# Images 1 to 3's scan inputs made on a clock, and two backward results kept apart in every phase

## The chip, the core and the metric

The kernel runs on one core of a Trainium2 chip. Its engines work side by side, each through its own instructions in order: PE (TensorE, matrix products), DVE (VectorE), ACT (ScalarE), POOL (GpSimd) and SP (SyncE, which here issues the DMAs). The metric is the device time of one execution in microseconds. Three runs of the kernel before gave 5556.42, 5560.28 and 5569.84 us; their median, 5560.28, is the time before.

## The reference

Four images of 64 x 64 positions with 96 channels go through four layers. What matters here is the first, a two-dimensional selective scan:

```python
xz = x @ W_in.T; xp, z = xz[..., :192], xz[..., 192:]
xc = silu(conv3x3(xp) + conv_b)                     # 192 -> 192 channels
xs = four orders of the 4096 positions: rows, columns, and both reversed
dts, Bs, Cs = split(x_proj(xs));  delta = softplus(dt_proj(dts) + dt_b)
h_t = exp(delta_t * A) * h_{t-1} + delta_t * u_t * B_t   # 192 channels x 16 states
y_t = sum over the 16 states of h_t * C_t
out = (sum of y over the four orders, + D * u) * silu(z) @ W_out.T
```

Then come a depthwise and a pointwise convolution, a linear attention with a quantised feed-forward, and a filter by Fourier transforms with another feed-forward. All of it is 32-bit but for the feed-forwards.

## The kernel before

**Scans.** A scan instruction of DVE runs the recurrence along 1024 positions (a chunk; four make an image) for 128 rows, which are 8 channels x 16 states. An image has 24 such groups (NG), a group is a unit, and a unit has two phases: the even one ("row") scans along rows, the odd one along columns, over a copy of B that ACT has turned (Bc, L1628). There are N = 192 phases and eight steps in each. In steps 0 to 3 chunks 0 to 3 are scanned forward into tiles S (L1959), in steps 4 to 7 chunks 3 to 0 backward (L1966). ACT makes the decays exp(delta * A) into two PSUM tiles "pa" just ahead (decay, L1669 and L1675): one each at steps 0 to 2 and at steps 5, 6 and 7.

A backward result can go two ways. As a rule it overwrites its decay in pa, and DVE adds it to the forward one (L1977), after a copy of its first column as the next chunk's start (L1976); POOL then multiplies the sum by C (times_c, L1658) and PE adds up the 16 states into PSUM (reduce, L1691: four matmuls of 512 columns for each chunk, as the profile counts them). For a chunk listed in apart[n] it goes into B's own tile instead, nothing is added, and POOL and PE treat it as a further result. At the unit's end ACT copies the one PSUM bank "py" out (L1698). The function plan(n) lays down at which step of the phase each of these is issued. Before the change apart[n] is (3,) as long as the flag "pre" is not set, and (3, 2) afterwards.

**Five S tiles** serve all phases in turn, so a forward scan waits until PE has reduced what stood there before. One step is 2.7 to 3.6 us.

**The other work** goes in between. After each step the function pieces(step) gives each engine a credit (gains, in estimated us: PE, ACT, POOL, DVE, SP) and lets the waiting streams issue while the credit lasts; streams are Python generators that yield the cost of what they issue next, NEXT (not before the next step) or LONG (only at step 12 of 16). clock[0] counts the steps. There are two lanes, served in this order. The side lane turns the column scans' results back (turn_back) and adds up an image's four orders (post: L648, L675). The main lane (main_lane) first makes the scan inputs of images 1, 2 and 3 one after the other, then sets done["pre"], then takes images 0, 1 and 2 through the other layers (rest). Image 0's inputs are made ahead of the scans. After the scans the lanes are emptied, and image 3's rest follows alone.

**The scan inputs** (before_scans) of an image are eight blocks of 512 positions, through five streams: project (load x, normalise on ACT in tile xb at L317, PE products into padded tiles "low" and "high"), project_z, convolve (30 products a block, L393), gates (silu and softplus on ACT; the two silus, at L508 and L509, stand behind LONG and need two loads of the activation table), and scan_inputs (four POOL operations for each half, L576 to L584, and the stores). Streams hold each other up by counts of finished blocks. While "pre" is not set the credits are multiplied by (0.9, 1.05, 1.25, 1, 1); in the last 24 phases, POOL's and SP's by 1.25.

**The rest of an image** in order: layer 1 (L937), layer norms (L1038 to L1108), attention (L1125, L1198), feed-forward (L1225, L1234, L1245), Fourier stages (L1299 and L1321, L1378, L1427, L1466), layer norm, feed-forward.

Of the kernel before, what the change touches and what calls it, by code (L numbers as in the profile page):

```python
# [24 lines left out]
NG = DI // 8  # L25
RK = 6
BLK = 512
NBLK = L // BLK
# [19 lines left out]
NCH = L // CH  # L48
NEXT = "next"
LONG = "long"  # L50


class Region:
# [20 lines left out]
def layers(ctx: ExitStack, tc: tile.TileContext, a: dict, out):  # L74
# [36 lines left out]
    clock = [0]  # L111
# [11 lines left out]
    def steps_past(since, n):  # L123

        while ordered[0] and clock[0] < since + n:
            yield NEXT
# [8 lines left out]
    done = {}  # L135
# [35 lines left out]
    def rows_of(i):  # L171

        r0 = RPB * i
        return r0, max(r0 - 1, 0), min(r0 + RPB + 1, HW)
# [40 lines left out]
    def until(ready):  # L215
        while not ready():
            yield NEXT
# [43 lines left out]
    def before_scans(b, wk, take, deep=1, prev=None):  # L261
# [5 lines left out]
        pairs = b == 0  # L267

        def count(stage):

            before = NBLK if prev is None else done[stage, prev]
            return done.get((stage, b), 0) + before - NBLK
# [18 lines left out]
        def project():  # L291

            yield from until(lambda: b in norm and count("z") > -2)
            gn = norm[b]

            def load_x(i):
                _, lo, hi = rows_of(i)
                xb = wk.tile([C, RPB + 2, HW], F32, tag="xb", name="xb", bufs=2)
                nc.sync.dma_start(
                    xb[:, : hi - lo, :],  # L300
                    x[:, lo * HW : hi * HW].rearrange("p (r w) -> p r w", w=HW),
                )
                return xb, clock[0]

            nxt = load_x(0)
            for i in range(NBLK):
                yield from until(
                    lambda: i - len(padded) < count("conv") and i - 2 < count("z")
                )
                r0, lo, hi = rows_of(i)  # L310
                n = hi - lo
                yield NEXT
                xb, since = nxt
                yield from steps_past(since, LANDING)
                yield (0, 0.9, 0, 0)
                xbs[b, i] = xb
                nc.scalar.activation(  # L317
                    xb[:, :n, :], xb[:, :n, :], AF.Identity, scale=gn[:, 0:1], bias=gn[:, 1:2]
                )
                low, high = xps[b, i] = padded[i % len(padded)]  # L320
                if i == 0 or i == NBLK - 1:
                    edge = 0 if i == 0 else RPB + 1
                    nc.gpsimd.memset(low[:, edge, :], 0.0)
                    nc.gpsimd.memset(high[: 128 if pairs else 64, edge, :], 0.0)
                at = lo - r0 + 1
                for c in range(2):
                    for ra, rb in ((0, 5), (5, n)):
                        p, give = yield from take("p_xp", 128, (rb - ra) * HW)
                        yield (0.8, 0, 0, 0)
                        nc.tensor.matmul(  # L330
                            p, lhsT=w_twice if c else w_in[:, :128], rhs=xb[:, ra:rb, :],
                            start=True, stop=True,
                        )
                        yield NEXT
                        yield (0, 0.84 if c else 0.42, 0, 0)
                        rows = p.rearrange("p (r w) -> p r w", w=HW)
                        if c == 0:
                            nc.scalar.copy(low[:, at + ra : at + rb, 1 : HW + 1], rows)
                        else:
                            nc.scalar.copy(high[:64, at + ra : at + rb, 1 : HW + 1], rows[:64])  # L340
                            if pairs:
                                nc.scalar.copy(
                                    high[64:, at + ra : at + rb, :HW], rows[64:]
                                )
                                give()
                                continue

                            ja, jb = max(at + ra - 1, 0), min(at + rb - 1, RPB)
                            nc.scalar.copy(
                                high[64:, ja:jb, 1 : HW + 1],  # L350
                                rows[64:, ja + 1 - at - ra : jb + 1 - at - ra, :],
                            )
                        give()
                done["project", b] = i + 1
                if i + 1 < NBLK:
                    yield from until(lambda: i - 1 < count("z"))
                    yield (0, 0, 0, 0, 1)
                    nxt = load_x(i + 1)
# [140 lines left out]
        def gates():  # L499

            for i in range(NBLK):
# [3 lines left out]
                sz = szs.pop((b, i))  # L505
                yield LONG
                flush()
# [1069 lines left out]
    N = 2 * len(units)  # L1577
    dls, Bs, Bcs, Ss, gs, reps, rep_cols = {}, {}, {}, {}, {}, {}, {}
    pys, yss = {}, {}
    apart = {}  # L1580

    def phase(n):

        b, g = units[n // 2]
        return b, g, n % 2
# [177 lines left out]
    def pieces(step):  # L1763

        clock[0] += 1
        assert clock[0] % 16 == (step + 1) % 16
        for free, bank in returned:
            free.append(bank)
        returned.clear()
        for e in range(5):  # L1770

            more = 1.25 if e in (2, 4) and clock[0] > 8 * (N - NG) else 1
            if "pre" not in done:
                more = (0.9, 1.05, 1.25, 1, 1)[e]
            credit[e] = min(cap[e], credit[e] + gains[step][e] * more)
        for lane in list(lanes):
            if not lane.live():
                lanes.remove(lane)
                continue
            for s in list(lane.streams):  # L1780
                while s[1] is not None:
                    if s[1] == NEXT:
                        if s[2] == clock[0]:
                            break
                        lane.advance(s)
                        continue
                    if s[1] == LONG:
                        if step != 12:
                            break
                        cost = (0, 5.0, 0, 0)  # L1790
                    else:
                        cost = s[1]
                        if any(
                            c > 0 and credit[e] < min(c, cap[e]) - 0.5 for e, c in enumerate(cost)
                        ):
                            break
                    for e in range(len(cost)):
                        credit[e] -= cost[e]
                    lane.advance(s)
                if s[1] is None:  # L1800
                    lane.streams.remove(s)
# [91 lines left out]
    def plan(n):  # L1893

        t, u = 8 * n, n // 2
        two = "pre" in done
        apart[n] = (3, 2) if two else (3,)
        row = n % 2 == 0
        b, g, _ = phase(n)
        last, first = g == NG - 1, g == 0  # L1900

        if row:
            for q, k in ((0, 7), (1, 8), (2, 9), (3, 10)):
                at(t + k, load_du, u + 1, q)
            for q, k in ((0, 3), (1, 5), (2, 15), (3, 16)):
                at(t + k, load_delta, u + 1, q)
            if last:
                for q in range(NCH):
                    at(t + 2 + q, load_rep, b + 1, 0, q)
                for q, k in ((3, 8), (2, 9), (1, 11), (0, 12)):  # L1910
                    at(t + k, load_rep, b + 1, 1, q)
            for q, k in ((3, 2), (2, 3), (1, 4), (0, 6)):
                at(t + k, copy_b, u, q)
            if first:
                for q in range(NCH):
                    at(t + 6 + q // 2, copy_rep, b, q)
        else:
            for q, k in ((0, 2), (1, 3), (2, 6 if two else 5), (3, 9)):
                at(t + k, times_b, u + 1, q)

        if two:
            order = ((2, False, 4, 6), (3, False, 5, 6), (3, True, 6, 7), (2, True, 7, 8))
        else:
            order = ((3, False, 4, 6), (2, False, 6, 7), (3, True, 7, 8))
        end = (0, False, 9, 10) if row else (0, False, 11, 12)
        for q, back, k, r in (*order, (1, False, 8, 9), end):
            at(t + k, times_c, n, q, back)
            at(t + r, reduce, n, q, back)
        if not row:
            at(t + 13, result, u)  # L1930
            for j in range(4):
                at(t + 14 + j, store_result, u, j)

    with tc.manual_schedule():
# [4 lines left out]
        for step in range(8 * N):  # L1939
            n, k = divmod(step, 8)  # L1940
            if k == 0:
                plan(n)
                if n % (2 * NG) == 2 * NG - 2 and n // 2 + 1 < len(units):
                    b = units[n // 2 + 1][0]
# [11 lines left out]
            if k < 4:  # L1956
                q = k
# [5 lines left out]
            else:  # L1963
                q = 7 - k
# [159 lines left out]
```

## Time and profile before

| | |
|---|---|
| median of three runs | 5560.28 us |
| profiled execution | 5556.72 us |
| its span | 5554.8 us |
| granted PE clock, mean | 0.805 |
| first to last scan | 290.6 to 5109.2 us |
| after the last scan | 445.6 us |
| adds at L1977 | 441 |
| backward scans into B / Bc | 163 / 164 |

The profile lists busy time by engine, groups of equal instructions with their count, busy time and mean, and the idle time ahead of them with what ended it ("POOL S L1658 <- DVE S L1959" is POOL waiting for the scan that writes S). A stretch is a window of the execution with each engine's busy time and number of instructions in it. Since every step has one scan, the number of scans started before an instruction gives its step, eight to a phase.

### The profile page before, as it was taken

Reading aid. Unit: us, or ns where it says so; the run is one execution under the profiler, and the core shown is the slowest. Engines: PE = TensorE matmul, PEld = TensorE weight load, DVE = VectorE, ACT = ScalarE, POOL = GpSimd, SP = SyncE. Lnnn points to the kernel's source line nnn. Section 1 sums busy time; section 2 is a strip of 40 time slices with the busy share of each in tenths; the row PEclk is TensorE's granted clock in tenths of the full one; section 3 lists DMA queues with packets and bytes.
Section 4 is the critical chain, followed back from the end, with each engine's and each line's share of the span. In section 5 each row is a group of like instructions: output and inputs, shape, how many; then the busy total and the mean of one; then the engine's idle time right before and its main releaser. Section 6 shows DMA issues by size and latency. Waiting matters only on the chain. (4 is left out here: it accounts for less than half of the span.)

```text
span 5554.8 us, 60794 instructions
## 1 busy us (share of the span) xinstructions
PE 4365.4 (79%) x20542; PEld 1597.5 (29%) x20542; DVE 4634.1 (83%) x3114; ACT 3563.4 (64%) x4542; POOL 3971.1 (71%) x1966
## 2 busy tenths in 40 slices
PE   7977888978888887787758876877478767786878
PEld 4422222222222221254202211542012213451346
DVE  4278988788778999999989999999899999997464
ACT  5767767777677567666675667576655676565233
POOL 1358777777777778878887789787887797786100
PEclk9978888988888877678768876797578867886888
DMA  4334443433355633436446434363465335463012
GB/s 128 97 110 115 115 123 107 135 114 115 113 148 157 184 100 92 120 114 194 135 136 181 119 96 120 113 197 107 135 175 152 97 101 165 149 182 109 7 56 95
DMA packets 298092, 694.68 MB, mean 125 GB/s; under 512 B 58184, under 2 KB 95156, under 8 KB 297652
## 3 DMA queue, kind: packets, MB, share of 16 engines
q1 hardware_dynamic: 297780, 690.80, 44.0%
q8 instruction: 162, 2.65, 0.2%
q14 instruction: 150, 1.23, 0.1%
HBM read 564.22 MB, written 126.35 MB: 124 GB/s over the span
## 5 line engine op out<-in xcount | busy, mean ns | idle before, releaser
L1658 POOL TENSOR_TENSOR S<-S,rep 128x1024 f32<-128x1024 f32 x768 | 1807.4, 2362 | 748.1 <-DVE S L1959 586.9
L1691 PE MATMUL py<-S,red 128*32 128x512 f32 x3072 | 947.6, 786 | 497.7 <-POOL S L1658 320.0
L1675 ACT ACTIVATE pa<-dl,nega 128x512 f32<-128x512 f32 x1152 | 791.1, 689 | 530.6 <-DVE Bc L1966 268.0
L1669 ACT ACTIVATE pa<-dl,nega 128x1024 f32<-128x1024 f32 x576 | 641.9, 1115 | 456.8 <-DVE S L1977 221.9
L1653 POOL TENSOR_TENSOR B<-B,rep 128x1024 f32<-128x1024 f32 x384 | 901.8, 2357 | 22.0 <-DMA B<-du_s 15.5
L1959 DVE TENSOR_TENSOR_SCAN S<-pa,S,Bc 128x1024 f32<-128x1024 f32 x288 | 676.0, 2347 | 179.3 <-PE py L1691 79.1
L1959 DVE TENSOR_TENSOR_SCAN S<-pa,S,B 128x1024 f32<-128x1024 f32 x288 | 676.0, 2347 | 142.1 <-ACT pa L1669 63.1
L1628 ACT COPY Bc<-B 128x1024 f32<-128x1024 f32 x384 | 747.7, 2009 | 16.2 <-POOL B L1653 11.9
L1977 DVE TENSOR_TENSOR S<-S,pa 128x1024 f32<-128x1024 f32 x441 | 535.9, 1215 | 6.6
L393 PE MATMUL p_conv<-low,conv_w 128*96 128x512 f32 x864 | 427.3, 647 | 31.3 <-ACT u L405 30.9
L1658 POOL TENSOR_TENSOR B<-B,rep 128x1024 f32<-128x1024 f32 x163 | 385.6, 2369 | 45.5 <-DVE pa L1966 22.4
L1691 PEld LDWEIGHTS py<-S,red 128*32 128x32 f32 x3072 | 118.8, 121 | 1036.1 <-POOL S L1658 580.8
L1966 DVE TENSOR_TENSOR_SCAN B<-pa,B 128x1024 f32<-128x1024 f32 x163 | 377.7, 2317 | 17.4 <-ACT Bc L1628 2.3
L1658 POOL TENSOR_TENSOR Bc<-Bc,rep 128x1024 f32<-128x1024 f32 x164 | 385.0, 2361 | 6.6 <-DVE Bc L1966 3.7
L1966 DVE TENSOR_TENSOR_SCAN Bc<-pa,Bc 128x1024 f32<-128x1024 f32 x164 | 379.3, 2313 | 4.5
L1966 DVE TENSOR_TENSOR_SCAN pa<-pa,edge,Bc 128x1024 f32<-128x1024 f32 x124 | 291.6, 2352 | 38.8 <-ACT pa L1675 38.8
L1234 POOL CAST h<-y 128x1536 fp8e5<-128x1536 f16 x64 | 96.0, 1500 | 305.0 <-ACT y L869 289.8
L1691 PE MATMUL py<-Bc,red 128*32 128x512 f32 x656 | 231.5, 809 | 104.1 <-POOL Bc L1658 104.0
L1966 DVE TENSOR_TENSOR_SCAN pa<-pa,edge,B 128x1024 f32<-128x1024 f32 x125 | 293.8, 2350 | 9.3 <-ACT pa L1669 9.2
L393 PE MATMUL p_conv<-high,conv_w 64*96 64x512 f32 (+1 forms) x576 | 274.7, 612 | 0.0
L1691 PE MATMUL py<-B,red 128*32 128x512 f32 x652 | 204.9, 709 | 61.8 <-POOL B L1658 61.8
L1966 DVE TENSOR_TENSOR_SCAN pa<-pa,B 128x1024 f32<-128x1024 f32 x96 | 226.1, 2356 | 26.3 <-ACT pa L1669 22.6
(274 smaller groups left out, 7409.2 us busy)
## 6 DMA issues: line engine op xcount, KB each, us to landing
dl<-delta_s SPq DMA_DIRECT2D x770, 256.0 KB
B<-du_s SPq DMA_DIRECT2D x768, 256.0 KB
z_s<-z SPq DMA_DIRECT2D x48, 512.0 KB
zl<-z_s SPq DMA_DIRECT2D x64, 384.0 KB
side<-y_s SPq DMA_DIRECT2D x112, 192.0 KB
rep<-bc_s SPq DMA_DIRECT2D x64, 256.0 KB
tw<-in_dft SPq DMA_DIRECT2D x64, 256.0 KB
side<-in_xT SPq DMA_DIRECT2D x64, 192.0 KB
```

Source lines behind the costliest of these rows:

```text
L393: nc.tensor.matmul(p, lhsT=conv_w[: src.shape[0], k, oc * C : (oc + 1) * C], rhs=src[:, ky : ky + RPB, kx : kx + HW], start=(k == 0), stop ...
L1234: nc.gpsimd.tensor_copy(h, y, saturate=False)
L1628: nc.scalar.copy(dst.rearrange("p (w h) -> p h w", h=HW)[:, q * h : (q + 1) * h, :], src.rearrange("p (h w) -> p h w", w=HW),)
L1653: nc.gpsimd.tensor_tensor(Bs[u, q], Bs[u, q], reps[units[u][0], 0, q], ALU.mult)
L1658: nc.gpsimd.tensor_tensor(t, t, c_of(n, q), ALU.mult)
L1669: nc.scalar.activation(pa, dls[u, q // 2][:, at : at + CH], AF.Exp, scale=scale)
L1675: nc.scalar.activation(to[:, k * HW // 2 : (k + 1) * HW // 2, :], src[:, :, q * w : (q + 1) * w], AF.Exp, scale=scale,)
L1691: nc.tensor.matmul(py[32 * j : 32 * j + 32, :], lhsT=red[:, 24 - 8 * s : 56 - 8 * s], rhs=x[:, k * BLK : (k + 1) * BLK], start=s == 0 and ...
L1959: nc.vector.tensor_tensor_scan(s, pas[q], b_of(n, q), Ss[n, q - 1][:, CH - 1 : CH] if q else 0.0, ALU.mult, ALU.add,)
L1966: nc.vector.tensor_tensor_scan(to[:, ::-1], pas[q][:, ::-1], b_of(n, q)[:, ::-1], edge if q < 3 else 0.0, ALU.mult, ALU.add,)
L1977: nc.vector.tensor_tensor(Ss[n, q], Ss[n, q], to, ALU.add)
```

## The change

- A constant PRE_STEPS = 470. In project, block i of image b (1 to 3) may not begin before step 470 x ((b - 1) x 8 + i) / 24, besides the conditions that it had.
- apart[n] is (3, 2) in every phase, and plan lays down the order of that case always.
- In the last 24 phases PE's credit too is multiplied by 1.25.

```diff
+PRE_STEPS = 470
...
             nxt = load_x(0)
             for i in range(NBLK):
+                turn_of = 0 if pairs else PRE_STEPS * ((b - 1) * NBLK + i) // (3 * NBLK)
                 yield from until(
                     lambda: i - len(padded) < count("conv") and i - 2 < count("z")
+                    and clock[0] >= turn_of
                 )
...
-            more = 1.25 if e in (2, 4) and clock[0] > 8 * (N - NG) else 1
+            more = 1.25 if e in (0, 2, 4) and clock[0] > 8 * (N - NG) else 1
             if "pre" not in done:
                 more = (0.9, 1.05, 1.25, 1, 1)[e]
...
         t, u = 8 * n, n // 2
-        two = "pre" in done
-        apart[n] = (3, 2) if two else (3,)
+        apart[n] = (3, 2)
...
-            for q, k in ((0, 2), (1, 3), (2, 6 if two else 5), (3, 9)):
+            for q, k in ((0, 2), (1, 3), (2, 6), (3, 9)):
                 at(t + k, times_b, u + 1, q)
 
-        if two:
-            order = ((2, False, 4, 6), (3, False, 5, 6), (3, True, 6, 7), (2, True, 7, 8))
-        else:
-            order = ((3, False, 4, 6), (2, False, 6, 7), (3, True, 7, 8))
+        order = ((2, False, 4, 6), (3, False, 5, 6), (3, True, 6, 7), (2, True, 7, 8))
```

(An entry of order is the chunk, whether it is the backward result, the step of POOL's multiply and the step of PE's reduction.)

## The prediction

> **What bounds the kernel now.** I read the page's first two parts, then a table of stretches cut at the starts of phases (a phase is eight scans on DVE; its start is the start of its first scan, which reads no S), then DVE's waits, then single stretches of the timeline.
>
> ```profile
> span 5554.8 us, 60794 instructions
> PE 4365.4 (79%) x20542; PEld 1597.5 (29%) x20542; DVE 4634.1 (83%) x3114; ACT 3563.4 (64%) x4542; POOL 3971.1 (71%) x1966
> ```
>
> No engine is full over the span. The stretches differ (columns: us, then busy us of PE, weight load, DVE, ACT and POOL, then PE clock and DMA):
>
> ```profile
> 404.30:711.70 307.40, 257.60 (x615) 68.38 (x614) 267.32 (x156) 226.64 (x286) 239.99 (x124) 0.84 0.41 117
> 711.70:1161.00 449.30, 392.57 (x938) 112.86 (x936) 356.46 (x210) 330.23 (x432) 338.82 (x178) 0.87 0.41 119
> 1366.00:1598.00 232.00, 205.07 (x481) 59.03 (x480) 178.15 (x105) 163.88 (x212) 169.86 (x89) 0.85 0.45 128
> 1743.90:1986.90 243.00, 192.92 (x502) 51.68 (x501) 228.38 (x144) 146.81 (x169) 197.64 (x93) 0.87 0.63 174
> 404.30:1986.90 1582.60, 1348.90 (x3241) 374.19 (x3240) 1319.87 (x780) 1135.90 (x1433) 1210.79 (x620) 0.86 0.45 129
> 1986.90:5109.20 3122.30, 2324.88 (x12978) 871.93 (x12976) 2911.85 (x1722) 2050.38 (x2545) 2553.74 (x1176) 0.76 0.48 134
> ```
>
> These are phases 4-15, 16-31, 40-47, 53-62, 4-62 and 63-191: 25.6, 28.1, 29.0, 24.3, 26.8 and 24.2 us a phase. From phase 63 on DVE is busy 93% and is the bound. Up to phase 56, while the inputs of images 1 to 3 are made, DVE is busy 22.3 us of 25 to 29 and waits for others:
>
> ```profile
> DVE S L1959 <- PE py L1691: 86.5, 31, 4.6
> DVE S L1959 <- ACT pa L1669: 75.8, 44, 23.2
> DVE pa L1966 <- ACT pa L1675: 38.1, 19, 4.0
> ```
>
> (290.6 to 1839.9 us.) The engines run in order, so PE's reductions stand behind the convolution, ACT's decays behind evacuations that wait for PE. In the dense stretch (phases 40-47) PE is busy 88%.
>
> **Where the input blocks lie.** Counting scans gives each row a step (eight a phase). The 24 blocks' first ACT rows (xb, L317) lie at steps 5, 10, 24, 42, 58, 81, 105, 126, then mostly 16 apart up to 398; the last POOL row of an input (L584) is at step 450. The flag is therefore set in phase 56: 441 adds at L1977 are 384 + 57, three in each of 57 phases and two in the other 135.
>
> **Part a, the clock.** Block j may not start before step 470j/24, so blocks come every 19.6 steps, the last at 450 or later; with the 52 steps from 398 to 450 the inputs end near step 502, phase 62. The wait is in the order of issue; no engine waits in it. Its DMAs, two PE stages, ACT and POOL work move with it, same number. Prices by stretch: phases 4-15 had blocks at 42, 58, 81, 105 and 126, 21 steps apart, and cost 25.6 us with (257.60 - 77.68)/12 = 15.0 us of PE other than the reductions (77.68 is line L1691's busy time there). Phases 16-31, 16 apart, cost 28.1 with (392.57 - 93.33)/16 = 18.7. A block is thus 39 us of PE; at 19.6 steps it is 39.2 x 8/19.6 = 16.0 a phase, and 25.6 + 1.0 x (28.1 - 25.6)/3.7 = 26.3 us. 59 phases (4 to 62) at 26.3 are 1552 against 1582.6: **-31**. At 25.6 it is -72; at the old 26.8, nothing.
>
> **Part b, two results apart.** In 57 phases one add goes, with its copy of the edge: a scan ended at 1384.63 and the next began at 1385.86, so 1.23 us, at most 70 in all. But ACT must have the next decay ready:
>
> ```profile
> 1413.89 1.21 DVE L1977 TENSOR_TENSOR S<-S,pa 128x1024 f32<-128x1024 f32 x1
> 1416.89 2.36 DVE L1966 TENSOR_TENSOR_SCAN pa<-pa,edge,Bc 128x1024 f32<-128x1024 f32 x1 [1.79 <-ACT pa L1675]
> ```
>
> Here ACT was in the two silus with their table loads (1410.83 to 1415.44), and without the add DVE would only wait longer. There is one such turn for each of 24 blocks, so 33 of 57 phases keep the gain: -41. Added are 57 POOL multiplies of 2.36 us (rows L1658) and 57 reductions, 1.33 us each ((231.5 + 204.9)/(656 + 652) a matmul, four to each), 76 us of PE. A block's PE time costs (28.1 - 25.6)/3.7 = 0.67 us per us with its ACT and POOL work; a reduction brings PE alone, so I take half, 0.33: +25. Zero and the full 76 are the ends. POOL's need becomes 20.0 + 2.36 + about 0.3 = 22.7 us a phase; it was busy 173.1 of 192.1 us (90%) at 3274.8 to 3466.9, at 24.0 us a phase, so it is no bound at 26: 0. The multiply of B's chunk 2 goes from step 5 to 6 of the odd phase, its scan comes four steps later: 0. B's chunk 2 is freed at step 8 instead of 5, and SP loads into it at step 10; later phases do the same with 8.5 us of such waits by POOL: 0; if the cover goes, SP's later loads queue behind it. Sum **-16**, ends -70 and +76.
>
> **Part c, what the inputs now meet.** Image 0's sums (L648, L675) run at steps 426 to 494. Until now the convolution (L393) ended at 426. Now three blocks fall among them. The sums cost 187.5 x 96/336 + 72.5 x 32/112 = 74 us of PE; 52 of their 62 steps now lie beside convolutions, 62 us. No row shows both. Alone on PE they would cost 0.33 a us, as a dense block 0.67; the middle gives **+31**, ends 0 and 47 (0.75, from phases 40-47).
>
> **Part d, image 0's layer 1** (L937, 68 us of PE: (128.5 + 75.6)/3) stood at steps 457 to 513, paced by the sums; it now starts near 503 with its input complete, and catches up. It ran partly in phases 57-62, which part a has priced anew, so some of its cost comes back: 0 to 23 (0.33), taken **+6**. The rest of the image ended at step 790 and image 1's began at 830, so a delay of up to 40 steps goes no further.
>
> **Part e, PE's 1.25 in the last 24 phases.** Image 2's Fourier stages ran slower there than image 1's: L1299 took 58 steps (1377-1435) against 43, beside image 3's sums. With a quarter more PE credit I expect some 20 steps back, which brings in what was left over at the end: four of its eight last feed-forward blocks ran after the scans, with 4.4 + 5.3 + 5.1 = 14.8 us of PE between 5107 and 5200 (L1225, L1245, L1108) while PE was 98% busy (24.44 of 25, 5150 to 5175). **-15**, and +3 for what the scans then carry; ends -20 and +10.
>
> **Sum**: -31 - 16 + 31 + 6 - 12 = -22 on the profiled execution's 5556.7 us (span 5554.8 and 1.9 around it), 5535. That execution lies 3.6 under the median of 5560.3: **5538 us**. A change within 0.3% (17 us) is what a measurement can hardly tell from none.
>
> **Rivals.** (1) *PE becomes the bound* (slower). Phases 4-62 hold 1348.9 us of PE, 355.8 of them L1691's; less the sums' 74 and some 40 of layer 1 the inputs are 879, and some 18 move in from phases 0-3. The new load is 897 + 74 + 59 x 7.45 of reductions (1006.0/135 phases, L1691 after 1839.9) = 1411 us. At the 85.2% that PE reached there (1348.9/1582.6) it takes 1655, +72; with d and e +66: **5626**. It decides below 89%. For it: 88% is the most that any long stretch of inputs held, and PE is what DVE waits for first. Against it: the 88% stood where the order of issue was crowded; at 21 steps 25.6 us sufficed.
>
> (2) *Everything takes.* 25.6 a phase (-72), all adds saved less the reductions (-45), no cost in c and d, -15: **5428**. Against it: the silu turns.
>
> (3) *No effect*: crowding goes from early phases to phases 53-62, and b nets nothing: **5560**, within 17.
>
> (4) *A colder PE.* The row first: after 6.2 us without work, 12 convolution matmuls took 8.02 us, 0.67 each; 6 soon after took 2.82, 0.47.
>
> ```profile
> 1385.66 1.92 PE L1691 MATMUL py<-S,red 128*32 128x512 f32 x4 [6.22 <-ACT ys L1698]
> 1387.51 2.02 PE L544 MATMUL p_dt<-xd,dt_w 6*96 6x512 f32 x2
> 1390.04 8.02 PE L393 MATMUL p_conv<-low,conv_w 128*96 128x512 f32 x12 [0.51 <-ACT u L405]
> 1397.99 1.05 PE L1691 MATMUL py<-S,red 128*32 128x512 f32 x4
> 1398.97 2.82 PE L393 MATMUL p_conv<-low,conv_w 128*96 128x512 f32 x6
> ```
>
> One more such gap a block costs 24 x 2.4 = 58 us of PE, at 0.67 +39: **5577**. Against it: at 21 steps a convolution matmul took 126.44/270 = 0.47 us busy at clock 0.84, in the dense stretch 119.82/240 = 0.50 at 0.85: spreading did not cool PE. The Trainium skill, "TensorE: Matmul & The Clock Gate", Part 1 (the HAM clock gate), says that one idle window of about 3.4 us brings the array back to half clock; by that rule each pause between blocks would be paid. The gap of 6.2 us agrees with it, the 21-step stretch does not show more such pauses.
>
> **Chances.** Forecast 0.38 (5470 to 5543); (2) 0.10; (3) 0.16; (1) 0.30; (4) 0.06. Faster is 0.48, same 0.16, slower 0.36. The range runs from 5455, halfway to (2), to 5640, a little over (1)'s price, and leaves out about half of (2) and the far part of (1).
>
> **What would show it.** L1977 has 384 rows and L1966's "B" and "Bc" forms 192 each. The xb rows lie near steps 20 apart and L584 ends near 502 (a: phases 16-47 at 26 to 26.5 us). DVE's waits for PE py fall below 86 us per 57 phases, and those for ACT pa at the backward scans rise (b). Phases 53-62 take 28 us or more (c); L937 starts near 503 (d); L1245 of image 2 ends by the last scan and the stretch after it is 12 to 18 us shorter (e). I am wrong if PE's share in phases 4-62 stays at 85% (rival 1), or if conv matmuls there exceed 0.50 us (rival 4).

## The result and the profile after

The changed kernel takes 5511.99 us (median of four runs, 5505.39 to 5519.88) against 5562.38 for the kernel before (four runs): ratio 0.9909, 95% interval 0.9891 to 0.9928. The forecast was 5538 us, in a range that holds the result; the gain is 50 us where 22 were forecast.

The profiled execution of after is its slowest run (5519.88 us). Its totals, busy time by engine and number of instructions:

```profile
span 5518.1 us, 61390 instructions
PE 4353.0 (79%) x20770; PEld 1587.4 (29%) x20770; DVE 4556.9 (83%) x2993; ACT 3556.7 (64%) x4549; POOL 4099.1 (74%) x2023
```

DVE does 77 us less (57 adds of 1.22 us and 57 edge copies of 0.16 us are gone), POOL 128 us more. PE has 228 more instructions and yet 12 us less busy time. The stretches of after, cut at the same phases (16-31, 40-47, 53-62, 4-62, 63-191, then the last 24 phases and the time after the scans; columns as before):

```profile
704.80:1104.20 399.40, 341.04 (x901) 94.21 (x899) 336.95 (x178) 301.95 (x383) 358.48 (x183) 0.89 0.45 128
1320.60:1523.20 202.60, 170.74 (x454) 47.01 (x450) 168.45 (x89) 145.62 (x182) 174.91 (x87) 0.90 0.50 141
1662.40:1918.50 256.10, 226.12 (x604) 64.10 (x602) 223.30 (x136) 173.35 (x213) 217.29 (x109) 0.91 0.60 165
405.50:1918.50 1513.00, 1296.56 (x3346) 352.29 (x3344) 1255.24 (x675) 1127.01 (x1417) 1325.09 (x669) 0.87 0.47 133
1918.50:5075.70 3157.20, 2372.99 (x13127) 885.00 (x13127) 2914.34 (x1727) 2057.84 (x2579) 2566.68 (x1185) 0.77 0.48 134
4483.50:5075.70 592.20, 456.00 (x3457) 212.93 (x3453) 552.52 (x333) 381.65 (x480) 467.62 (x211) 0.77 0.50 144
5075.70:5518.10 442.40, 355.08 (x3285) 200.04 (x3285) 208.35 (x317) 123.06 (x212) 47.04 (x52) 0.83 0.18 58
```

The dense stretches are where the time went: 449.3 us became 399.4 in phases 16-31, 232.0 became 202.6 in phases 40-47. Phases 53-62, which took the displaced blocks, went from 243.0 to 256.1. Some is given back behind them: phases 63-191 take 35 us longer. By stretches the two spans differ by +8.1 ahead of the scans (no instruction of the change lies there, and that stretch varies from 290.5 to 299.0 us between kernels that are the same in it), -6.9 in phases 0-3, -69.6 in 4-62, +19.0 in 63-167, +16.0 in the last 24 and -3.3 after the scans: -36.7 in the profiles. The medians show more because the profiled run of after is the slowest of its four and that of before is under its median.

DVE's waits in phases 4-62, before and then after (who waited, for whom; us in all, times, longest):

```profile
DVE S L1959 <- PE py L1691: 89.1, 33, 4.6
DVE S L1959 <- ACT pa L1669: 51.8, 43, 2.9
DVE pa L1966 <- ACT pa L1675: 36.9, 19, 4.0
DVE S L1959 <- ACT pa L1675: 26.5, 18, 3.2
...
DVE pa L1966 <- ACT pa L1669: 3.8, 4, 1.6
```

```profile
DVE S L1958 <- ACT pa L1678: 71.8, 49, 6.1
DVE S L1958 <- PE py L1694: 44.8, 24, 5.3
DVE pa L1965 <- ACT pa L1678: 36.0, 19, 5.5
DVE S L1958 <- ACT pa L1672: 32.4, 19, 3.9
DVE pa L1965 <- ACT pa L1672: 24.5, 16, 2.8
```

Waiting for PE halved, 89.1 to 44.8; waiting for ACT's decays rose from 119.0 (51.8 + 36.9 + 26.5 + 3.8) to 164.7. Two questions follow: why did the clock bring so much more than priced, and what took most of the 57 saved adds?

### The profile page after: what moved, and what is told of

It reads as the page before. It is cut to its first block, busy times and chain, and to the rows that moved or that the text cites. A ratio compares the mean times of both kernels' runs of the same rounds, so it can differ in the third digit from the quotient of the medians.

```text
span 5518.1 us, 61390 instructions
## 1 busy us (share of the span) xinstructions
PE 4353.0 (79%) x20770; PEld 1587.4 (29%) x20770; DVE 4556.9 (83%) x2993; ACT 3556.7 (64%) x4549; POOL 4099.1 (74%) x2023
## 3 DMA queue, kind: packets, MB, share of 16 engines
q14 instruction: 152, 1.25, 0.1%
## 5 line engine op out<-in xcount | busy, mean ns | idle before, releaser
L1694 PE MATMUL py<-S,red 128*32 128x512 f32 x3072 | 889.8, 777 | 460.6 <-POOL S L1661 356.3
L1656 POOL TENSOR_TENSOR B<-B,rep 128x1024 f32<-128x1024 f32 x384 | 902.2, 2357 | 32.2 <-DMA B<-du_s 29.4
L1958 DVE TENSOR_TENSOR_SCAN S<-pa,S,B 128x1024 f32<-128x1024 f32 x288 | 676.0, 2347 | 158.8 <-ACT pa L1672 48.2
L1661 POOL TENSOR_TENSOR B<-B,rep 128x1024 f32<-128x1024 f32 x192 | 453.5, 2365 | 76.9 <-DVE pa L1965 37.2
L1976 DVE TENSOR_TENSOR S<-S,pa 128x1024 f32<-128x1024 f32 x384 | 467.0, 1216 | 6.6
L1965 DVE TENSOR_TENSOR_SCAN B<-pa,B 128x1024 f32<-128x1024 f32 x192 | 444.9, 2317 | 20.0 <-ACT Bc L1631 4.4
L1661 POOL TENSOR_TENSOR Bc<-Bc,rep 128x1024 f32<-128x1024 f32 x192 | 449.9, 2358 | 8.8 <-DVE pa L1965 8.0
L1965 DVE TENSOR_TENSOR_SCAN Bc<-pa,Bc 128x1024 f32<-128x1024 f32 x192 | 445.0, 2318 | 5.6
L396 PE MATMUL p_conv<-low,conv_w 128*96 128x512 f32 x864 | 412.9, 623 | 4.2 <-ACT u L408 4.2
L1694 PE MATMUL py<-Bc,red 128*32 128x512 f32 x768 | 264.6, 779 | 125.6 <-POOL Bc L1661 125.2
L1694 PE MATMUL py<-B,red 128*32 128x512 f32 x768 | 249.6, 743 | 68.5 <-POOL B L1661 68.5
L396 PE MATMUL p_conv<-high,conv_w 64*96 64x512 f32 (+1 forms) x576 | 271.0, 607 | 0.0
L1965 DVE TENSOR_TENSOR_SCAN pa<-pa,Bc 128x1024 f32<-128x1024 f32 x96 | 226.1, 2355 | 53.4 <-ACT pa L1678 47.8
L1958 DVE TENSOR_TENSOR_SCAN S<-pa,B 128x1024 f32<-128x1024 f32 x96 | 219.0, 2281 | 28.6 <-ACT pa L1672 28.6
```

Source lines behind the costliest of these rows:

```text
L396: nc.tensor.matmul(p, lhsT=conv_w[: src.shape[0], k, oc * C : (oc + 1) * C], rhs=src[:, ky : ky + RPB, kx : kx + HW], start=(k == 0), stop ...
L1656: nc.gpsimd.tensor_tensor(Bs[u, q], Bs[u, q], reps[units[u][0], 0, q], ALU.mult)
L1661: nc.gpsimd.tensor_tensor(t, t, c_of(n, q), ALU.mult)
L1694: nc.tensor.matmul(py[32 * j : 32 * j + 32, :], lhsT=red[:, 24 - 8 * s : 56 - 8 * s], rhs=x[:, k * BLK : (k + 1) * BLK], start=s == 0 and ...
L1958: nc.vector.tensor_tensor_scan(s, pas[q], b_of(n, q), Ss[n, q - 1][:, CH - 1 : CH] if q else 0.0, ALU.mult, ALU.add,)
L1965: nc.vector.tensor_tensor_scan(to[:, ::-1], pas[q][:, ::-1], b_of(n, q)[:, ::-1], edge if q < 3 else 0.0, ALU.mult, ALU.add,)
```

## Experiments: one part at a time

**The clock alone.** The kernel before with only the constant and the condition in project:

```diff
+PRE_STEPS = 470
+                turn_of = 0 if pairs else PRE_STEPS * ((b - 1) * NBLK + i) // (3 * NBLK)
+                    and clock[0] >= turn_of
```

> The clock alone: blocks wait for step 470j/24, but only one backward result is kept apart while the inputs are made, and PE's credit stays as before. Theory A (the two parts pay separately): the step of the prediction holds, phases 4 to 62 take about 1550 us instead of 1582.6, and with the meeting of sums and convolution the time is 5530 to 5560. Theory B (they pay only together: the clock frees ACT and PE, the second result apart turns that into shorter phases): phases 4 to 62 take 1560 to 1580 and the time is within 15 us of the kernel before, 5545 to 5575. Theory C (the clock does most of it): phases 4 to 62 near 1525, time near 5515.

5529.35 us, ratio 0.9931 [0.9910, 0.9952]: most of the gain. The stretches of phases 4-51 and 52-62 in before, then with the clock alone:

```profile
404.30:1716.40 1312.10, 1131.02 (x2690) 315.78 (x2688) 1069.17 (x624) 966.92 (x1239) 996.45 (x520) 0.86 0.42 121
1716.40:1986.90 270.50, 217.88 (x551) 58.41 (x552) 250.69 (x157) 168.98 (x194) 214.34 (x101) 0.86 0.60 167
```

```profile
409.60:1654.00 1244.40, 1055.98 (x2518) 286.40 (x2516) 1069.55 (x626) 932.27 (x1179) 975.17 (x502) 0.86 0.44 124
1654.00:1934.80 280.80, 243.12 (x595) 66.30 (x594) 257.90 (x168) 195.14 (x238) 214.62 (x110) 0.88 0.59 165
```

Phases 4-51 lose 67.7 us, phases 52-62 gain 10.3: -57 where the prediction had -31 + 31 = 0 for a and c. In all, phases 4-62 take 1525.2 us, as theory C of the expectation had it. DVE's work in 4-51 is the same (1069.2 and 1069.6 us), so all of it is waiting that went away.

**Two results apart alone.** The kernel before with

```diff
-        two = "pre" in done
+        two = True
```

> Two backward results apart in every phase, blocks as early as before, PE's credit as before. Theory A: 25 to 40 us faster, 5522 to 5537, phases 4 to 56 at 26.2 to 26.5 us instead of 26.9. Theory B: in the dense stretch DVE waits for ACT and PE as long as it has saved, phases 36 to 51 stay at 28.5 or more, and the time is within 15 us of the kernel before or slower, 5550 to 5590. Theory C: no gain, 5560.

5553.26 us, 0.9978 [0.9965, 0.9990]. Phases 4-62 with it, to be read against the same stretch of before in the prediction (1582.60 us):

```profile
403.90:1980.50 1576.60, 1345.40 (x3454) 372.78 (x3453) 1254.46 (x674) 1134.38 (x1433) 1334.06 (x675) 0.87 0.45 129
```

DVE has 65.4 us less to do and the stretch is 6.0 us shorter; POOL has 123.3 us more. Nearly all of the saved work turned into waiting. The 6.0 us themselves are not more than two profiles of one program can differ by: the credit alone, the next experiment, changes nothing ahead of phase 168, and its profile has 1575.8 us in this stretch. The medians (12 runs against 23) do show a gain: 15 us, 6 to 19 by the interval. PE took 213 more matmuls, 71 us at the prediction's 0.33 us each, and was busy 3.5 us less than before and 4.8 us more than with the credit alone, so its busy time is no fixed demand that can be added up.

**The credit alone.** The kernel before with `e in (0, 2, 4)` in pieces.

> Only PE's credit times 1.25 in the last 24 phases. The prediction's step: 12 us faster, 5548, the stretch after the last scan 12 to 18 us shorter, phases 168 to 191 at most 3 us longer. Rival: what the stretch after the scans saves (3 us in the changed kernel's profile) is less than what the last 24 phases lose to a fuller PE (16 us there), and the time is 5565 to 5580.

5575.02 us, 1.0016 [1.0003, 1.0028]: the wrong side. The last 24 phases and the time after them:

```profile
4538.10:5128.60 590.50, 454.54 (x3457) 215.15 (x3453) 552.20 (x333) 381.47 (x480) 466.93 (x211) 0.78 0.50 146
5128.60:5567.30 438.70, 353.04 (x3285) 198.54 (x3285) 208.16 (x317) 123.18 (x211) 47.44 (x52) 0.85 0.17 57
```

Against before (576.2 and 445.7 us), 14.3 us are lost while the scans run and 7.0 are won behind them.

**All but the credit.** The changed kernel with `e in (2, 4)` put back.

> The changed kernel without PE's 1.25. If the credit gains 12 us, this takes 5524, 12 more than the changed kernel's 5512. Rival: it takes 5495 to 5505, because phases 168 to 191 go back to 576 us while the stretch after the scans grows by 3 to 9 us. Phases 4 to 62 stay near 1513 us under both.

5512.53 us, 0.9896 [0.9879, 0.9913], beside 0.9909 [0.9891, 0.9928] with the credit. The intervals overlap; the stretches agree with the experiment before: 578.8 us in the last 24 phases where the changed kernel has 592.2, and 445.9 after them where it has 442.4. This kernel is the base of what follows. In phases 4-62 it takes 1513.1 us, the clock alone 1525.2: b is worth 12 us beside the clock, and 17 by the medians (5529.35 and 5512.53, with intervals that just touch).

How far single profiles can be trusted shows where kernels are the same program up to phase 51: phases 4-51 take 1312.1 us in before and 1303.0 with the credit alone, and 1234.6 to 1239.4 in the four kernels of this text that are the base there. A difference of less than some 10 us between two profiles is therefore not shown by them. In phases 63-167 the spread is wider: the eleven kernels here whose layers stand at the base's steps take 2551 to 2573 us, the three that stand as in before 2546 to 2553.

## Experiments: the pace, and the sums

The base with PRE_STEPS 384, 430 and 510 in place of 470:

> Clock over 384 steps (16 a block, the old dense pace) with two results apart, PE's credit as before. Theory P (what pays is the pace: a block costs less DVE idle time when it has 19.6 steps instead of 16): the dense stretches return, phases 16 to 51 at 28 us, and the time is that of two results apart alone, near 5553. Rival Q (what pays is that blocks stand at even places, at any pace): phases 16 to 51 at 26 us or less and a time of 5520 or less.

> Clock over 430 steps (17.9 a block), else as the run before. P: between the 384 and the 470 steps, near 5530; the inputs end some 40 steps earlier than with 470, so image 0's layers start earlier and phases 63 to 143 lose some 10 us less. If the later start of image 0's layers costs as much as the denser blocks, the time is within 8 us of that with 470 steps (5512).

> Clock over 510 steps (21.3 a block). P: phases 4 to 51 at 25 us or less, some 20 us under the 1235 of 470 steps; but one and a half more blocks fall beside image 0's sums and its layers start some 40 steps later, so phases 52 to 167 take 15 to 35 us more: 5505 to 5530. If the sums beside the convolution cost as the prediction priced it (0.5 us for each us of the sums' PE), it is slower than 470 steps by 15 us or more.

And the base at 470 with image 0's sums held back until all inputs are made:

```diff
-        yield from until(lambda: ("scans" if 1 in halves else "half", b) in done)
+        yield from until(
+            lambda: ("scans" if 1 in halves else "half", b) in done and "pre" in done
+        )
```

> Clock over 470 steps and two results apart, PE's credit as before, but image 0's sums wait until the inputs of images 1 to 3 are done, so the two no longer meet. If their meeting costs what step c of the prediction says (31 us), phases 52 to 62 fall from 278 us to 250 or less. Rival: the credits already share PE between them, the meeting costs 10 us or less, phases 52 to 62 take 268 or more, and image 0's layers come later still, so that the time rises to 5515 to 5535.

| | median us | ratio to before | phases 4-51 | rows a phase there | 52-62 | 63-167 | after the scans |
|---|---|---|---|---|---|---|---|
| before | 5571.84 | 1 | 1312.1 | 26.8 | 270.5 | 2546.0 | 445.7 |
| 384 | 5545.55 | 0.9961 [0.9943, 0.9978] | 1308.9 | 27.5 | 263.4 | 2537.2 | 442.6 |
| 430 | 5544.27 | 0.9948 [0.9931, 0.9965] | 1283.6 | 26.4 | 278.1 | 2553.7 | 445.9 |
| 470 | 5512.53 | 0.9896 [0.9879, 0.9913] | 1234.7 | 24.2 | 278.4 | 2571.7 | 445.9 |
| 510 | 5606.16 | 1.0064 [1.0047, 1.0081] | 1187.5 | 22.6 | 293.9 | 2614.2 | 531.0 |
| 470, sums later | 5619.01 | 1.0086 [1.0071, 1.0101] | 1239.4 | 24.2 | 262.3 | 2609.7 | 533.0 |

(Rows are the convolution's matmuls, counted in the traces. The base at 470 ran beside another set of runs of before, with a median of 5568.51.)

Two things follow. Up to phase 51 the gain grows with every step that the blocks are spread further: 27.3, 26.7, 25.7 and 24.7 us a phase, 0.47 to 0.60 us for each row less. At 384 the blocks stand as evenly as at 470 and the stretch is as long as in before. So the clock acts through the load and not through even places or some lucky phase. And there is a cliff, which the expectation for 510 (5505 to 5530) did not see: with 510, or with the sums late, image 0's layer 1 ends at step 586 (554 at 470) and its last feed-forward runs at steps 857 to 919 (799 to 839), beside image 1's sums; image 1's layer 1 begins at 923 (845), and the last of image 2's Fourier stages and its last feed-forward fall out of the scans. Phases 63-167 lose 38 to 43 us more than at 470, and the time after the scans grows by 85 to 87.

The run with the sums held back also prices part c directly: phases 52-62 take 262.3 us without image 0's sums and 278.4 with them, 16 us, where 31 were forecast. (One pair of profiles; their phases 4-51, the same program, differ by 4.8.)

To buy back part of what phases 63-167 lose, PE got 1.15 of its credit while image 0's rest runs, at 470 and at 500:

```diff
+            if e == 0 and 480 < clock[0] < 860:
+                more = 1.15
```

> Clock over 470 steps, two results apart, and PE's credit times 1.15 at steps 481 to 859, where image 0's layers run late, instead of 1.25 in the last 24 phases. If the 26 us that phases 63 to 167 lost against the kernel before come from the late start of image 0's layers, which runs into image 1's sums, then the last feed-forward of image 0 (794 to 839 without it) ends at 825 or earlier, those phases take 2572 - 10 to 20 us, and the time falls to 5495 to 5505. Rival: more PE credit makes DVE wait, as in the last 24 phases (+14 us there), and the time stays at 5510 to 5525.

> As the run before with a clock over 500 steps. With 510 steps phases 4 to 51 took 1188 us (1235 with 470) but image 0's layers ended at step 919, image 1's and 2's came late, and the stretch after the scans grew by 85 us. If the credit brings image 0's end to 860 or earlier, that stretch stays under 455 us, phases 4 to 51 take about 1200, and the time is 5480 to 5500. If not, it is as slow as with 510 steps, 5570 to 5610.

5520.13 us (0.9913 [0.9884, 0.9941]) and 5549.19 (0.9956 [0.9938, 0.9973]). At 470 image 0's last feed-forward ended at 829 instead of 839, but phases 57-95 took 973.6 us (base 958.5) and phases 96-143 gave back 12.0 (1172.5 against 1184.5). Neither beats the base.

## Experiments: what took the adds

The base saves DVE 58.6 us of work in phases 4-51 over the clock alone (1069.55 against 1010.92 busy), and the stretch is 9.7 us shorter. Three suspects were relieved in turn, each time in both kernels, so that the difference of a pair is what b brings without that suspect.

**ACT's table loads** (the suspect of the prediction). For images 1 to 3 both silus become Identity, and the return to the exponential's table is left out:

```diff
-                nc.scalar.activation(u, u, AF.Silu)
-                nc.scalar.activation(sz, sz, AF.Silu)
-                natural_exp()
+                act = AF.Silu if b == 0 else AF.Identity
+                nc.scalar.activation(u, u, act)
+                nc.scalar.activation(sz, sz, act)
+                if b == 0:
+                    natural_exp()
```

> The clock alone over 470 steps (one result apart while inputs are made), and the two silus of images 1 to 3 are replaced by a plain copy through the same engine, so that the two loads of the activation table in each block (2.57 us of ACT) are left out; the output is therefore another one. Reference for the next run. ACT has 62 us less to do in all: phases 4 to 51 some 10 to 30 us under the 1244 of the clock alone, and the idle time of DVE ahead of the scan of step 14 of 16, 0.54 us a unit there, falls to under 0.2.

> As the run before, with two results apart in every phase. If the silus with their table loads are what takes the second result's gain (step b of the prediction: one phase of two keeps nothing), then without the loads the gain over the run before is 40 us or more in phases 4 to 51, against 10 with them (1244.4 to 1234.7), and DVE's idle time ahead of step 14 stays under 0.4 us a unit instead of 1.34. Rival: ACT and PE are late at other steps as well, the gain stays at 10 to 25 us, and idle time at steps 2, 6, 7 and 10 takes the rest.

Clock alone 5495.29 us (0.9866 [0.9840, 0.9893]), both 5503.26 (0.9877 [0.9845, 0.9909]): by the medians b brings nothing here. Phases 4-51 take 1229.3 and 1222.7 us, a difference of 6.6. DVE's idle time ahead of the scan at step 6 of the odd phase, two steps behind the place of the silus, falls from 1.34 to 0.20 us a unit with both; the idle time ahead of all scans is still 4.34 us a phase, against 3.24 for its pair (4.59 and 3.54 with the tables). So the gain of b did not grow: the silu turns alone are not what holds it back.

**PE.** The convolution of images 1 to 3 does 2 of its 15 products for each half:

```diff
+                        if k not in (0, 14):
+                            continue
```

> The clock alone over 470 steps, and of the 15 products of each convolution result of images 1 to 3 only the first and the last are issued; the order and the credits of everything else are unchanged, the output is another one. Some 600 us of PE fall away in phases 0 to 60. Reference for the next run. If PE's lateness is what the inputs' phases wait for, phases 4 to 51 fall from 1244 us to 1150 or less (24 us a phase; DVE is busy 22.3), and DVE's waits for ACT's decays fall with its waits for PE, because ACT stands behind evacuations that wait for PE. If the handing over of the two decay tiles between ACT and DVE is slow by itself, they stay above 1200.

> As the run before, with two results apart in every phase. DVE has 59 us less to do in phases 4 to 51. Theory L (with PE late, ACT is late, and DVE's saved time turns into idle time): with PE no longer late the gain over the run before is 35 to 59 us in phases 4 to 51, against 10 with the whole convolution and 7 without the table loads. Theory M (two decay tiles alone cause it): the gain stays under 20 us and DVE's idle time rises by 35 us or more as before.

5397.11 us (0.9695 [0.9672, 0.9717]) and 5375.63 (0.9659 [0.9633, 0.9685]). Phases 4-51, clock alone and both:

```profile
404.50:1532.90 1128.40, 752.53 (x1506) 138.82 (x1502) 1067.96 (x626) 932.06 (x1179) 974.03 (x501) 0.66 0.48 137
```

```profile
396.40:1536.10 1139.70, 760.95 (x1700) 140.25 (x1700) 1009.30 (x529) 931.62 (x1179) 1084.80 (x550) 0.69 0.48 135
```

With PE out of the way b makes this stretch 11.3 us *longer*, or at the least brings nothing in it. (By the medians b brings 21 us here, but not in phases 4-62, which take 1399.9 and 1401.8 us; the profiles have it behind them, 2572.6 and 2551.2 us in phases 63-167, the two ends of that stretch's spread.) In the first DVE is busy 95%; in the second it has 58.7 us less to do, and POOL is busy 95% (1084.80 of 1139.70). POOL's waits in the two stretches, clock alone and then both:

```profile
POOL S L1662 <- DVE S L1963: 78.0, 25, 5.8
POOL S L1662 <- DVE S L1981: 68.5, 31, 3.8
```

```profile
POOL S L1662 <- DVE S L1959: 42.9, 19, 6.2
```

POOL no longer waits for DVE's sums. DVE waits 12.7 us for POOL itself in phases 4-62 with both, but 84.0 for ACT's decays, against 28.4 with the clock alone. By which way POOL's load reaches ACT the waits do not tell; that it does, the next pairs show.

**POOL.** In scan_inputs two of the four operations of each half are left out for images 1 to 3 (`w = w - e` and `r = r - w` only `if b == 0`), once with the short convolution and once with the full one:

> The clock alone with the short convolution, and of POOL's four operations for each half block of images 1 to 3 two are left out (w - e and r - w, 1.27 us each; delta lacks their correction). POOL has 112 us less to do in phases 4 to 62. Reference for the next run: DVE is busy 1068 us in phases 4 to 51 and was 95% busy there, so they stay at 1115 to 1130 us.

> As the run before with two results apart. Theory K (POOL took over as the bound: with the short convolution it was busy 1084.8 of 1139.7 us, 95%, with hardly a wait): with POOL's need down from 22.6 to 20.7 us a phase the second result now gains 30 to 55 us in phases 4 to 51 over the run before, against -11 with all of POOL's work. Theory M (the two decay tiles): the gain stays under 15 us.

> The clock alone with the whole convolution and POOL's two operations left out. Reference for the next run. DVE does not wait for POOL here, so phases 4 to 51 stay within 15 us of the 1244 of the clock alone.

> As the run before with two results apart. If POOL's load is what takes the second result's gain in the kernel as it is (POOL busy 88% in phases 4 to 51), the gain over the run before is 30 us or more in phases 4 to 51 instead of 10. If PE's and ACT's lateness take it, as long as the convolution is whole, it stays at 5 to 20 us.

Short convolution: 5396.98 us (0.9692 [0.9673, 0.9711]) and 5341.11 (0.9601 [0.9578, 0.9623]). Full: 5512.61 (0.9906 [0.9887, 0.9926]) and 5485.73 (0.9855 [0.9836, 0.9874]). Phases 4-51 of the first pair:

```profile
404.30:1529.40 1125.10, 724.89 (x1506) 136.15 (x1502) 1067.88 (x625) 931.00 (x1179) 878.23 (x424) 0.68 0.49 137
```

```profile
398.40:1496.20 1097.80, 726.05 (x1699) 136.31 (x1698) 1009.31 (x530) 929.54 (x1179) 989.71 (x472) 0.71 0.50 141
```

| phases 4-51 | clock alone | both | what b brings |
|---|---|---|---|
| full convolution | 1244.4 | 1234.7 | -9.7 |
| full, less POOL | 1237.3 | 1219.4 | -17.9 |
| short convolution | 1128.4 | 1139.7 | +11.3 |
| short, less POOL | 1125.1 | 1097.8 | -27.3 |

Relieving POOL is worth little to the clock alone (3.3 to 7.1 us) and 15 to 42 us to the kernel with both. POOL's extra multiplies are thus a real price of b where PE does not limit: 39 us of its gain. In the real kernel it is 8 us, which is within the spread of single profiles; by the medians b brings 27 us with POOL relieved and 17 without, and the intervals leave open whether that differs. In phases 4-62 the short pair differs by 35.9 us and the full pair by 18.0.

It is not the whole price. With PE and POOL both relieved 27.3 of 58.6 us arrive in phases 4-51. DVE's waits for ACT's decays in phases 4-62 of this last pair, clock alone and then both:

```profile
DVE pa L1972 <- ACT pa L1681: 10.6, 8, 2.7
DVE S L1965 <- ACT pa L1681: 9.0, 12, 1.5
...
DVE S L1965 <- ACT pa L1675: 1.6, 5, 0.4
```

```profile
DVE pa L1968 <- ACT pa L1681: 21.8, 9, 3.9
DVE S L1961 <- ACT pa L1681: 17.0, 26, 2.5
...
DVE S L1961 <- ACT pa L1675: 6.4, 7, 2.6
...
DVE pa L1968 <- ACT pa L1675: 3.0, 2, 2.5
```

They go from 21.2 to 48.2 us. In these phases DVE has 72.3 us less to do and the pair differs by 35.9, so 27 of the missing 36 us stand here. The same holds in the real pair: DVE's idle time ahead of its scans grows by 2.1 us a unit, and 1.46 of them lie ahead of the three scans at steps 6 and 7 of the even and step 6 of the odd phase, at or just behind the place of the removed add.

The traces name what ACT did just before. In phases 4-62 DVE waited for a decay 65 times with the clock alone (97.8 us) and 99 times in the base (166.1 us). In none of these did the decay wait for its tile: each time ACT came to it, or to the run of decays that it stands in, straight from another instruction, with a pause of 12 ns at most. Two of them, ACT and DVE in the base:

```profile
443.83 1.28 ACT L108 ACT_TABLE_LOAD   x1
445.12 2.75 ACT L1678 ACTIVATE pa<-dl,nega 128x512 f32<-128x512 f32 x4
446.57 2.36 DVE L1965 TENSOR_TENSOR_SCAN pa<-pa,Bc 128x1024 f32<-128x1024 f32 x1 [3.89 <-ACT pa L1678]
```

```profile
488.96 0.68 ACT L408 ACTIVATE u<-p_conv,conv_b 96x512 f32<-96x512 f32 x1 [5.27 <-PE p_conv L396]
489.54 1.40 ACT L1678 ACTIVATE pa<-dl,nega 128x512 f32<-128x512 f32 x2
491.03 2.35 DVE L1958 TENSOR_TENSOR_SCAN S<-pa,S,Bc 128x1024 f32<-128x1024 f32 x1 [4.91 <-ACT pa L1678]
```

| the ACT instruction ahead of the late decay | clock alone | base |
|---|---|---|
| table load after the silus (L108) | 16.3 | 35.9 |
| softplus (L560) | 17.3 | 33.8 |
| the convolution's evacuation, ACT's copy out of PSUM (L408), mostly itself late for PE | 17.3 | 27.5 |
| evacuation of z (L379) | 4.2 | 12.6 |
| a block's beginning (tiles xb, low and high) | 40.7 | 52.6 |

All of them grow. Without the table loads little is left of their row (4.3 us with both, behind the copies in their place), and the sum still grows by 51.6 us (90.1 to 141.7) where it grew by 68.3 with them; the row of softplus then goes from 17.3 to 40.6. So no single instruction takes the adds. A reading that fits, but that no run tested, is that the add between two scans was also time in which ACT could catch up. A third pa tile, which would let ACT run further ahead, was not tried.

## Why the prediction was right or wrong, point by point

**Direction and range** came out; the size did not: 50 us where 22 were forecast. The step that failed is the load in part a: with the rows that the trace counts, its own slope gives -66 us where it forecast -31. The price of c is the second.

**a, forecast -31 and c, +31; measured together -57** (-51 against the profile of the credit alone, where before is the same program). The slope of the two stretches was sound, the load put on it was not: 59 phases were charged a block every 19.6 steps, 24.5 rows of the convolution a phase (the profile counts 60 to a block). But 24 blocks are all there are; some rows ran ahead of phase 4 and the convolution ended at step 477, before phase 60. Counted in the trace, phases 4-51 hold 24.2 a phase and phases 52-62 only 16.4. The same two points of before (25.62 us at 22.5 rows, 28.08 at 29.2, 0.367 us a row) then give 48 x 26.24 + 11 x 23.38 = 1517, -66 and not -31. Rival (1) had the right total at hand: 897 us of PE where part a used 59 x 16.0 = 944. The rest is smaller: phases 4-51 came 15 us under the line (25.92 us a phase against 26.24), for which no run gives the reason, and phases 52-62 are 24 over it where c had 31 (16 by the run with the sums held back): -66 - 15 + 24 = -57, as measured. c let the sums and the convolution add up at near a dense block's rate. That was too dear, it seems because in part they only took longer: the sums ran at steps 425 to 502 (426 to 493 before) and the inputs ended at 514, not 502.

**b, forecast -16; measured -15 alone and -17 beside the clock by the medians**, -6 and -12 in phases 4-62 of single profiles. That the size came out is luck, since its terms did not. "The silu turns eat 24 of 57" fell: without table loads b brings no more. "POOL: 0", because it stood 90% busy in another stretch at 24.0 us a phase, was wrong: where PE does not limit, relieving POOL adds 39 us to b. The 25 us for PE's reductions are not confirmed: with POOL relieved, b brings 17.9 us beside the full convolution and 27.3 beside the short one, and the 9.4 us between them are no more than the spread of profiles. Right was the sentence that ACT must have the next decay ready; it holds for all of ACT's work, not for the silus alone.

**d, forecast +6 (0 to 23); measured +26 in phases 63-167** (base 2571.7 against 2546.0, clock alone 2572.2) and +19 in the changed kernel. These are the dear end of the spread: the eleven kernels with the base's steps average 2562 us and the three with those of before 2549, +13. Layer 1 began at step 521 and not 503. Image 0's rest ended at 839, 49 steps later than 790, past the 40 steps of slack: image 1's layer 1 began at 845 instead of 830. The slack was read rightly and then used up by the inputs' own delay; the pace of 510 shows what lies behind it.

**e, forecast -12; measured +7 alone** by stretches (+14.3 while the scans run, -7.0 behind them), 0.16% by the medians. Two of the four left-over feed-forward blocks came in (of the first product's rows, L1225 before and L1228 after, 12 stood behind the scans and 6 do now), and the scans carried them at twice the price. Both terms were mis-sized: the +3 "for what the scans then carry" measured 14, and the -15 behind them -7.

**The rivals.** (1) did not come, though its sign did: PE's share in phases 4-62 stayed at 85.7% (1296.56 of 1513.00). The prediction said that this share would make it wrong; that test was bad, since the rival counted 1411 us of PE and PE was busy only 1297. A share says nothing of the time when the busy time itself moves. (4) did not come either: the granted clock in 4-62 went from 0.86 to 0.87, and a convolution matmul took 0.475 us busy ((412.9 + 271.0)/1440; before (427.3 + 274.7)/1440 = 0.488). At the prediction's gap the granted clock was indeed 0.50, from 1381.7 to 1395.4 us of before. The Trainium skill, "TensorE: Matmul & The Clock Gate", Part 1 (the HAM clock gate), has one idle window of about 3.4 us bring the array back to half clock. The traces agree at that gap, and by the two means above spreading brought no more of it. (2) had a nearly right: -72, where the clock alone less 16 for the sums gives -73; its other terms were wrong. (3) is excluded: the interval puts the gain at 40 us or more.

**The signs.** L1976 has 384 rows and the B and Bc backward scans 192 each; the input blocks begin at steps 5, 20, 41, 58, 78, 104 and so on, some 20 apart; the waits for PE fell, those for ACT rose. Phases 16-31 take 24.96 us and not 26 to 26.5, phases 53-62 25.6 and not 28, and the time after the scans is 3.3 us shorter and not 12 to 18.

## What to carry to other kernels

When work is spread, count the load of each stretch in instructions before a slope is put on it, and see that the stretches add up to the work that there is; a wrong count cost this forecast 35 us, more than any of the prices that it did not know. Time saved on an engine that waits for others is worth what the next late engine leaves: relieve the suspects one at a time in both versions, and read the difference of each pair. A pace that is better with each step can have a cliff right behind it, where a late stage meets the next image's; look for the slack of what stands downstream before the last step.

## What the runs showed of the hardware that was not expected

PE's busy time is not the sum of its instructions at fixed prices. With two results apart alone, 3454 matmuls in phases 4-62 were busy 1345.4 us where 3241 were busy 1348.9 in one profile and 1340.6 in another of the same program, at granted clocks of 0.87, 0.86 and 0.86; with the whole change 3346 took 1296.6, at 0.87. With the short convolution the granted clock of phases 4-51 fell to 0.66 to 0.71.

A POOL multiply of S took 2353 ns (median, phases 4-51) in the kernel before and 2352 ns where POOL was busy 95% of the stretch beside DVE (both results apart, short convolution): the price of b on POOL is the queue, not a slower instruction.

The stretch ahead of the scans took 290.5 to 299.0 us in kernels that are the same there; the runs do not tell why, and differences of a few us between single profiles were read by stretch for that reason.
